# Small results of the first graph layer: one PSUM bank taken once, its halves handed out in turn

## The chip, the cores and the metric

The kernel runs on one core of a Trainium2 chip. The metric is the device time of one execution in microseconds. The engines are TensorE (PE in the profile, its weight loads PEld), VectorE (DVE), ScalarE (ACT), GpSimd (POOL) and SyncE (SP). PSUM, the memory into which TensorE writes, has eight banks of 128 partitions by 512 numbers of 4 bytes.

## The reference

Four layers work on x, 6250 nodes by 256, each with a layer norm ahead of it and a residual around it. The change lies in the first, a graph layer over 106250 edges that come sorted by their target:

```python
def _L0_gnn_ref(x, edge_index, edge_attr, u, batch, W1, b1, W2, b2):
    row, col = (edge_index[0], edge_index[1])
    h = jnp.concatenate([x[row], edge_attr], axis=1)
    h = jax.nn.relu(h @ W1 + b1)
    agg = jax.ops.segment_sum(h, col, num_segments=N_NODES)
    cnt = jax.ops.segment_sum(jnp.ones((h.shape[0],), h.dtype), col, num_segments=N_NODES)
    agg = agg / jnp.maximum(cnt, 1.0)[:, None]
    out = jnp.concatenate([x, agg], axis=1)
    return jax.nn.relu(out @ W2 + b2)
...
x = x + _L0_gnn_ref(_layernorm(x, axis=-1), edge_index, edge_attr_256, ...)
x = x + _L0_ffn_ref(_layernorm(x, axis=-1)[None], ...)[0]   # graph attention, then experts
x = x + _L1_gnn_ref(_layernorm(x, axis=-1), edge_weight, ...)
x = x + _L1_ffn_ref(_layernorm(x, axis=-1)[None], ...)
```

For each edge the hidden vector is relu(x[source] W1a + attribute W1b + b1). Each node takes the mean of its edges' hidden vectors, multiplies itself and the mean with W2, and adds the result to x.

## The kernel before

**Tiling.** The nodes stand in 49 blocks of 128 (`w`), seven blocks to a batch. As the edges are sorted by target, a block's edges are a window of consecutive ones. A window is worked on in three groups (`NG`) of six chunks (`G1`) of 128 edges, so the first layer's main loop runs over 147 groups `q`.

**Ahead of the loop** the product x W1a + b1 of every node is written to DRAM (`y_dram`), so that an edge only needs the row of its source. The layer's keys for a sort that the last graph layer wants, and the index windows of later batches, are made beside the loop.

**A group.** `load_sources(q)` has GpSimd gather the six chunks' rows of `y_dram` into a ring of four buffers `h` (L1128). `load_attr` fetches the attributes `ea` (L1399), and `turn` transposes them on VectorE into `et` (L1490). `hidden(q, j)` has TensorE multiply two chunks of `et` by `w1b` into `ph` (L1115, 128 x 1536 numbers, three banks). `join(q)` adds `ph` to the gathered rows on VectorE (L1508) and takes the relu on ScalarE (L1509). `add_up(q)` sums the edges per node: a 0/1 matrix `eq` (L1225) times `h`, accumulated over the window's three groups in `pe` (L1523, L1531), with a column of ones that counts the edges.

**The end of a block** is the generator `end_of(w)`. It is put in the list `work` once the block's last group has been summed, and each call of `steps` lets it go on to its next `yield`. In order:

- the count is inverted and the mean `ag` (a tile `o`) evicted from `pe` (L1541, L1542, L1544);
- `transposed` turns `ag` with two transposes by TensorE into a small PSUM tile `pt` (L1109) and evicts it on ScalarE (L1110);
- four Matmults with `w2` fill the next `pt` (`pm`; L1115, `pt<-w,b_all` and `pt<-w,o`), and VectorE adds the bias (L1556) and updates `x_all`, with the layer norm's statistics behind it;
- ScalarE writes the normed rows `xn` (L1572; also a tile `o`), which are turned in the same way into `b_all`;
- two Matmults with `wgx` give 24 numbers for each node (`pg`, `pt<-wgx,b_all`), the scores and values of the next layer, which ScalarE evicts in three pieces: `gtab` (L1583, L1584) and `a_dst` (L1585).

**Order.** Within one round of the loop the order is written out by hand, and `Ordered.pin()` keeps every engine's instructions in program order:

```python
if 0 < q <= NQ1: join(q - 1)
if q < NQ1: hidden(q, 0)
steps(sort)
if q >= 2: add_up(q - 2)   # every third q: work.append(end_of(...))
...                        # load_sources(q + 2), turn(q + 1)
if q < NQ1: hidden(q, 2)
steps()
if q < NQ1: equals[q] = equal(...); hidden(q, 4)
steps(slow)
```

So `steps` is called three times in a round, and nine times in a block. `end_of` has eleven pieces: the score product of block w comes one call ahead of the transposes of block w+1's mean, with the two chunks of one `hidden` (four Matmults) between them.

**PSUM.** Two buffers of `ph` take six banks, `pe` takes one, and the pool `p1`, with one buffer, the last. Every small result of the loop takes the tile `pt` of that pool: the four of `end_of`, the totals of `find_starts` (L1035), the two index transposes of `load_windows` (L1153), and in `sorted_edges` five transposes of keys (L1322), whose tile is [P, 4, P]. The three helpers get the pool as an argument and only call its `tile`. Which instruction must wait for which is worked out from the tiles' addresses and the pool's reuse when the program is built; the semaphores are put in there.

Of the kernel before, what the change touches and what calls it, by code (L numbers as in the profile page):

```python
# [1 line left out]

# [6 lines left out]
F32 = mybir.dt.float32  # L9
# [4 lines left out]
PSUM = bass.MemoryType.PSUM  # L14
DRAM = bass.MemoryType.DRAM

P = 128
# [4 lines left out]
def spread(n):  # L22

    cuts = [n] if n % 16 == 0 else [n // 16 * 16, n]
    return list(zip([0, *cuts[:-1]], cuts))


class Ordered:

    def __init__(self, tc):  # L30
        self.tc, self.last = tc, {}
        self.traced = tc.nc.cur_bb.bb.instructions
        self.at = self.traced[-1]
# [22 lines left out]
def general_path(ctx: ExitStack, tc: tile.TileContext, a: dict, out: bass.AP):  # L56
# [75 lines left out]
    def node_parts(ap, t0, t1):  # L132

        full = ap[0 : FULL * T, :].rearrange("(p t) d -> p t d", t=T)
        for p0, p1 in spread(FULL):
            yield slice(p0, p1), slice(t0, t1), full[p0:p1, t0:t1, :]
        if REST > t0:
            t2 = min(t1, REST)
            rest = ap[FULL * T + t0 : FULL * T + t2, :].rearrange("(o t) d -> o t d", o=1)
            yield slice(FULL, FULL + 1), slice(t0, t2), rest  # L140
# [728 lines left out]
def kernel(ctx: ExitStack, tc: tile.TileContext, a: dict, out: bass.AP):  # L869
# [10 lines left out]
    N, D = a["x"].shape  # L880
# [51 lines left out]
    def near_blocks(g):  # L932

        k = g * G + G / 2
        mid = k * (N / KM) / P
        spread_of = (C2 * (k / C2) * (1 - k / C2)) ** 0.5 * (N / KM) / P
        n = min(NK, int(-(-2 * (4.2 * spread_of + 0.9) // 1)))
        b0 = min(max(round(mid - n / 2), 0), T - 2)
        return b0, min(max(round(mid - n / 2) + n, b0 + 2), T) - b0
# [4 lines left out]
    with ExitStack() as fast:  # L944
# [51 lines left out]
        if T1 > C1:  # L996
            V.memset(flat.bitcast(I32)[:, C1:T1], 2**24)
            n = E1 - C1 * P
# [50 lines left out]
        def node_parts(ap, t0, t1):  # L1049

            t2 = min(t1, T - 1)
            if t2 > t0:
                rows = ap[t0 * P : t2 * P, :].rearrange("(t p) d -> p t d", p=P)
                yield slice(0, P), slice(t0, t2), rows
            if t1 == T:
                for p0, p1 in spread(LAST):
                    rows = ap[(T - 1) * P + p0 : (T - 1) * P + p1, :]
                    yield slice(p0, p1), slice(T - 1, T), rows.rearrange("p (o d) -> p o d", o=1)
# [248 lines left out]
        def sorted_edges(pst, wk):  # L1307

            k = order.bitcast(I32)[:, 0:KT]
            V.tensor_scalar(src2, k[:, 0:KA], 8191, None, op0=OP.bitwise_and)  # L1310
            some = key[:, 0:KT]
            for v, s in ((high, 20), (low, 13)):
                vi = some.bitcast(I32)
                V.tensor_scalar(
                    vi, k, s, 127, op0=OP.logical_shift_right, op1=OP.bitwise_and
                )
                V.tensor_copy(some, vi)
                V.tensor_scalar(some, some, -1.0, 127.0, op0=OP.mult, op1=OP.add)
                V.tensor_copy(v, some)
            for c in range(KA // P):  # L1320
                pt = pst.tile([P, 4, P], F32, name="pt")
                TE.transpose(pt[:, 0, :], some[:, c * P : (c + 1) * P], ident)  # L1322
                lt = wk.tile([P, P], BF16, name="lt")
                SC.activation(lt, pt[:, 0, :], AF.Copy)
                SC.dma_start(low_dram[c * P : (c + 1) * P, :], lt)
            V.tensor_add(good2[:, 1:2], good3[:, 0, 0:1], good3[:, 1, 0:1])
            V.tensor_add(good2[:, 3:4], good3[:, 0, 1:2], good3[:, 1, 1:2])

            lim = key[:, 0:KA]
            for g in range(KA // G):  # L1330
                V.memset(lim[:, g * G : (g + 1) * G], float(near_blocks(g)[0]))
            hit = order[:, 0:KA]
            V.tensor_tensor(hit, high[:, 0:KA], lim, op=OP.is_ge)
            for g in range(KA // G):
                V.memset(lim[:, g * G : (g + 1) * G], sum(near_blocks(g)) - 0.5)
            V.tensor_tensor(lim, lim, high[:, 0:KA], op=OP.is_ge)
            V.tensor_mul(hit, hit, lim)
            V.tensor_reduce(good2[:, 0:1], hit, axis=AX.X, op=OP.add)
# [5 lines left out]
        with ExitStack() as layer:  # L1344
# [114 lines left out]
            with (  # L1459
# [1 line left out]
                tc.tile_pool(name="y0", bufs=1) as wy,  # L1461
                tc.tile_pool(name="ph1", bufs=2, space=PSUM) as psh,
                tc.tile_pool(name="pe1", bufs=1, space=PSUM) as pse,
                tc.tile_pool(name="p1", bufs=1, space=PSUM) as psm,
            ):

                ring = [wy.tile([P, G1, HS], F32, name=f"h{i}") for i in range(4)]
                for h in ring:
                    V.memset(h[:, :, D:WS], 1.0)
# [134 lines left out]
                def sorting():  # L1604

                    yield from sort_steps()
                    sorted_edges(psm, wk)
# [151 lines left out]
        with (  # L1759
# [484 lines left out]
            k = NA + 5  # L2244
# [14 lines left out]
        with (  # L2259
# [297 lines left out]
            k = 0  # L2557
# [21 lines left out]
        with (  # L2579
# [6 lines left out]
            n = wk.tile([P, NB + 7], F32, name="n")  # L2586
# [4 lines left out]
            for i in range(2):  # L2591
                k = NB + 1 + 2 * i
# [55 lines left out]
```

## Time and profile before

| | |
|---|---|
| three runs | 4157.3, 4181.16, 4193.34 us; median 4181.16 |
| the profiled execution's own time | 4184.73 us |
| its span | 4182.9 us |
| granted TensorE clock, mean over the span | 0.857 |
| TensorE busy | 3303.4 us, 79% of the span |
| VectorE, GpSimd, ScalarE busy | 51%, 54%, 27% |

The profile shows one execution. Its times are microseconds from the span's start unless marked ns. "Idle before" is the time in which an engine stood ahead of an instruction, and the name behind the arrow is what ended it: an engine and line, a DMA, "issue" (it waited for nothing that the profile shows) or "remote" (an event that can't be tied to an instruction of this core). A float32 Matmult of the program stands in the trace as two records.

### The profile page before, as it was taken

The numbers are of one execution on the slowest core, as the hardware profiler recorded it, in microseconds if no ns is written. First come the engines' busy times: TensorE is split into PE (matmuls) and PEld (weight loads), VectorE is DVE, ScalarE is ACT, GpSimd is POOL, SyncE is SP. The second block draws the span as 40 slices with busy tenths as digits, with TensorE's granted clock in tenths as the row PEclk, the third lists the DMA queues.
The fourth block names the chain that finished last, engine by engine and source line by source line (L and its number), as shares of the span: only waits on it lengthen the run. The fifth ranks groups of instructions, "written<-read, shape, count | busy, mean of one in ns | idle before, by whom it ended". The sixth has DMA issues, their size and how long they took to land.

```text
span 4182.9 us, 57093 instructions
## 1 busy us (share of the span) xinstructions
PE 3303.4 (79%) x18509; PEld 2578.7 (62%) x18509; DVE 2138.8 (51%) x5571; ACT 1127.3 (27%) x2014; POOL 2249.3 (54%) x2364
## 2 busy tenths in 40 slices
PE   6888888898898885888898998786256866767788
PEld 5566666666576664677787777674245544555566
DVE  6566566665554444656455657555223333333344
ACT  4122222222222222333434344452001211111123
POOL 0656556566565634455454545534666666666651
PEclk8899999999899997999999999896557677767778
DMA  5677777777676742323333334333111111111210
GB/s 174 158 176 167 163 168 168 162 169 163 154 176 164 168 109 53 82 66 89 88 81 101 97 85 111 72 77 95 44 47 49 51 50 49 51 49 51 53 50 20
DMA packets 699200, 428.56 MB, mean 102 GB/s; under 512 B 531305, under 2 KB 640348, under 8 KB 698893
## 3 DMA queue, kind: packets, MB, share of 16 engines
q0 software_dynamic: 89408, 178.08, 18.4%
q1 hardware_dynamic: 366236, 187.21, 16.9%
q10 hardware_dynamic: 243248, 59.52, 7.2%
q8 instruction: 150, 2.46, 0.3%
q14 instruction: 158, 1.29, 0.1%
HBM read 382.05 MB, written 42.49 MB: 101 GB/s over the span
## 4 chain that ended last, share of the span: by engine, by line
PE 50%; another core or an unknown queue 18%; DVE 7%; issue 6%; ACT 3%; DMA 1%; POOL 0%; SPq 0%; ACTq 0%; DVEq 0%
PE ph L1115 22%; PE py L1115 10%; PE pe L2513 5%; PE pt L1115 4%; PE po L1873 4%; PE pe L1531 3%; PE pa L1810 1%; DVE eq L2492 1%; PE pt L1109 1%; DMA rb<-low_dram 1%; ACT hh L1709 1%; PE pe L2508 1%; ACT L1709 0%; DVE x_all L2054 0%
## 5 line engine op out<-in xcount | busy, mean ns | idle before, releaser
L1128 POOL DMA_INDIRECT h<-y_dram,src x882 | 846.6, 960 | 666.5 <-issue 508.4
L1128 POOL DMA_INDIRECT hg<-hp_dram,src x831 | 785.7, 946 | 457.8 <-issue 229.1
L1128 POOL DMA_INDIRECT sg<-gat_dram,src x640 | 612.0, 956 | 623.0 <-DVE px L1845 339.0
L1115 PE MATMUL ph<-w1b,et 128*128 128x256 f32 x3528 | 863.3, 397 | 35.9 <-issue 25.7
L1115 PEld LDWEIGHTS ph<-w1b,et 128*128 128x128 f32 x3528 | 677.5, 197 | 205.3 <-issue 115.9
L2513 PE MATMUL pe<-eq,hg 128*128 128x96 f32 (+15 forms) x2036 | 372.6, 331 | 158.3 <-issue 100.6
L2513 PEld LDWEIGHTS pe<-eq,hg 128*128 128x128 f32 x2036 | 359.0, 250 | 224.9 <-issue 157.8
L1508 DVE TENSOR_TENSOR h<-ph,h 128x1536 f32<-128x1536 f32 x147 | 258.2, 1757 | 428.8 <-remote 149.4
L1115 PE MATMUL py<-w,hh 128*128 128x256 f32 x1568 | 408.4, 400 | 64.2 <-ACT hh L1709 33.7
L1115 PE MATMUL ph<-b_all,w 128*128 128x256 f32 (+1 forms) x1600 | 417.1, 400 | 11.3 <-issue 9.8
L2492 DVE TENSOR_SCALAR eq<-px,dst,ew 128x96 f32<-128x96 f32 x831 | 262.3, 372 | 319.3 <-remote 137.4
L1509 ACT ACTIVATE h<-h 128x1536 f32<-128x1536 f32 x147 | 218.2, 1485 | 725.4 <-DMA ea<-in_edge_attr_dram 293.2
L1115 PEld LDWEIGHTS py<-w,hh 128*128 128x128 f32 x1568 | 300.3, 199 | 118.1 <-ACT hh L1709 41.7
L1115 PEld LDWEIGHTS ph<-b_all,w 128*128 128x128 f32 x1600 | 307.8, 202 | 55.4 <-issue 16.6
L1531 PE MATMUL pe<-h,eq 128*32 128x257 f32 x3168 | 257.2, 412 | 41.2 <-issue 40.9
L1873 PE MATMUL po<-pp,B 128*128 128x240 f32 (+10 forms) x1280 | 261.1, 344 | 17.2 <-DVE acc L1879 7.1
L1709 ACT ACTIVATE hh<-ph,b 128x256 f32<-128x256 f32 (+1 forms) x400 | 165.7, 466 | 392.0 <-remote 151.0
L1490 DVE STREAM_TRANSPOSE et<-ea 128x1536 f32<-128x1536 f32 x147 | 260.5, 1773 | 13.1 <-issue 9.5
L1873 PEld LDWEIGHTS po<-pp,B 128*128 128x128 f32 x1280 | 220.4, 194 | 32.0 <-issue 8.4
L1531 PEld LDWEIGHTS pe<-h,eq 128*32 128x32 f32 x3168 | 106.1, 115 | 148.0 <-issue 100.9
L1115 PE MATMUL py<-ew,g 65*128 65x256 f32 x392 | 136.5, 474 | 68.2 <-DVE x_all L2468 58.2
L1852 DVE TENSOR_TENSOR pp<-px,A 128x960 f32<-128x960 f32 (+10 forms) x160 | 156.3, 977 | 39.9 <-remote 27.5
(339 smaller groups left out, 3808.8 us busy)
## 6 DMA issues: line engine op xcount, KB each, us to landing
ea<-in_edge_attr_dram ACTq DMA_DIRECT2D x588, 96.0 KB
ea<-in_edge_attr_dram SPq DMA_DIRECT2D x588, 96.0 KB
y<-y SPq DMA_DIRECT2D x196, 128.0 KB
w<-in_L_ffn_W_dram SPq DMA_DIRECT2D x48, 512.0 KB
y<-ys SPq DMA_DIRECT2D x96, 256.0 KB
rb<-low_dram SPq DMA_DIRECT2D x80, 256.0 KB
h<-y_dram,src POOLq DMA_INDIRECT x882
hg<-hp_dram,src POOLq DMA_INDIRECT x831
```

The source lines that it names most:

```text
L1109: TE.transpose(pt[:, c, :], src[:, c * P : (c + 1) * P], ident)
L1115: TE.matmul(dst, lhs(c), rhs(c), start=c == 0, stop=c == n - 1)
L1128: GP.indirect_dma_start(out=dst, out_offset=None, in_=table[0:NP, :], in_offset=IndirectOffsetOnAxis(ap=idx, axis=0),)
L1490: V.transpose(et[q].rearrange("p c m k -> p m c k"), ahead.pop(q).rearrange("p i m (c k) -> p (i m) c k", c=2),)
L1508: V.tensor_add(h, ph.pop(q), h)
L1509: SC.activation(h, h, AF.Relu)
L1531: TE.matmul(sums[w][b * Q : (b + 1) * Q, :], eq[k][:, j, at], h[:, i * NT + j, 0:WS], start=g == 0 and j == NT - 1, stop=g == last_of[b] a ...
L1709: SC.activation(hidden[u][:, f, :n, :], ph[:, f - f0, :n, :], AF.Gelu, bias=b1[:, e, f : f + 1],)
L1852: V.tensor_tensor(pps[g, half][:, :, 0:n, :], pay[:, js, :].unsqueeze(2).to_broadcast([P, HG, n, HV]), near[g][:, js, 0:n].unsqueeze(3).to ...
L1873: TE.matmul(po.rearrange("p b v -> p (b v)"), B[:, j, :], pp[:, j, 0:n, :].rearrange("p b v -> p (b v)"), start=half == 0 and j == 0, stop ...
L2492: V.tensor_scalar(equals[k][:, j, :], lanes[:, 0:NW], dst_of[:, t : t + 1], ew[:, t : t + 1], op0=OP.is_equal, op1=OP.mult,)
L2513: TE.matmul(sums[b][:, lo - t0 * P : hi - t0 * P], hg[:, j, :], eq[:, j, lo - n0 : hi - n0], start=False, stop=after >= (t0 + n) * P,)
```

## The change

The pool `p1` gets the name `pends`. A new class `Halves` takes one tile of that pool, [P, 2, 256], and stands in for it as `psm`. Its `tile` hands out the first half, the second, the first again, and so on. A request for more than 256 numbers for each partition would get the whole bank. For no request to be so long, the tile of `sorted_edges` goes from [P, 4, P] to [P, 2, P]. All lines behind it move down by 18 or 19, so L1109 becomes L1127.

```diff
+class Halves:
+
+    def __init__(self, pool, width):
+        self.width, self.last = width, 1
+        self.bank = pool.tile([P, 2, width], F32, name="pt")
+
+    def tile(self, shape, dtype, name):
+        n = math.prod(shape[1:])
+        assert dtype == F32 and n <= 2 * self.width
+        if n > self.width:
+            v = self.bank.rearrange("p a k -> p (a k)")[:, 0:n]
+        else:
+            self.last = 1 - self.last
+            v = self.bank[:, self.last, 0:n]
+        return v if len(shape) == 2 else v.rearrange("p (c k) -> p c k", c=shape[1])
...
-                pt = pst.tile([P, 4, P], F32, name="pt")
+                pt = pst.tile([P, 2, P], F32, name="pt")
                 TE.transpose(pt[:, 0, :], some[:, c * P : (c + 1) * P], ident)
...
                 tc.tile_pool(name="ph1", bufs=2, space=PSUM) as psh,
                 tc.tile_pool(name="pe1", bufs=1, space=PSUM) as pse,
-                tc.tile_pool(name="p1", bufs=1, space=PSUM) as psm,
+                tc.tile_pool(name="p1", bufs=1, space=PSUM) as pends,
             ):
 
+                psm = Halves(pends, D)
                 ring = [wy.tile([P, G1, HS], F32, name=f"h{i}") for i in range(4)]
```

More of the change, by code (lines that the diff above doesn't have):

```diff
@@ L1 @@
+import math
 from contextlib import ExitStack
```

## The prediction

> **What bounds the kernel now.** I read the page's chain of waits first, then the table of stretches, then, for the first layer alone, TensorE's groups of instructions, the waits of all engines, and last the timeline around one of the places where TensorE stands.
>
> ```profile
> ## 4 chain that ended last, share of the span: by engine, by line
> PE 50%; another core or an unknown queue 18%; DVE 7%; issue 6%; ACT 3%; DMA 1%; POOL 0%; SPq 0%; ACTq 0%; DVEq 0%
> ```
>
> ```profile
> core 0: us, PE busy (x) PEld busy (x) DVE busy (x) ACT busy (x) POOL busy (x), PEclk, DMA share, GB/s
> 0.00:150.00 150.00, 103.39 (x441) 75.21 (x442) 92.39 (x309) 47.53 (x111) 30.55 (x39) 0.86 0.63 170
> 150.00:1540.00 1390.00, 1203.10 (x7395) 898.79 (x7394) 802.89 (x1556) 317.69 (x530) 816.73 (x851) 0.93 0.72 163
> ...
> ```
>
> The changed lines run in the second stretch: 1390.00 us of a span of 4182.9. There TensorE (PE) is busy 1203.10 us, 87%, at a granted clock of 0.93; no other engine reaches 60%. So the first layer is bound by TensorE, and a change to buffers can touch only the 187 us in which it stands. Half of the whole chain is TensorE's work, and the second entry, 18%, is time ended by an event that the trace can't tie to an instruction; the same word ("remote") comes back in the rows below.
>
> ```profile
> line engine op names shapes xcount | busy us, mean ns | idle before us <-releasers
> L1115 PE MATMUL ph<-w1b,et 128*128 128x256 f32 x3435 | 837.8, 395 | 26.3 <-issue 25.7
> L1531 PE MATMUL pe<-h,eq 128*32 128x257 f32 x3120 | 250.6, 411 | 31.6 <-issue 31.3
> ...
> L1109 PE MATMUL pt<-ident,o 128*128 128x128 f32 x192 | 40.8, 297 | 81.0 <-remote 47.5 <-ACT a_dst L1585 24.1 <-issue 4.2
> L1115 PE MATMUL pt<-wgx,b_all 128*128 128x24 f32 x188 | 26.1, 258 | 21.8 <-DVE dst L1170 10.6 <-issue 7.0 <-ACT b_all L1110 1.6
> ```
>
> The figures behind the bar are TensorE's idle time just ahead of the group. The largest, 81.0 us, stands ahead of the transposes into the bank of small results, which the change divides. Two entries make up most of it:
>
> ```profile
> PE pt L1109 <- remote: 47.5, 8, 9.2
> ...
> PE pt L1109 <- ACT a_dst L1585: 24.1, 4, 8.6
> ```
>
> That is 71.6 us in 12 places of 4 to 9 us. They are transposes of the mean of block w+1, and a_dst is ScalarE's last read of block w's score product from the same bank. One of the 12 in the timeline:
>
> ```profile
> 1482.89 0.52 PE L1115 MATMUL pt<-wgx,b_all 128*128 128x24 f32 x4
> ...
> 1483.26 1.97 PE L1115 MATMUL ph<-w1b,et 128*128 128x256 f32 x8
> ...
> 1493.25 0.18 ACT L1583 ACTIVATE gtab<-pt 128x16 f32<-128x16 f32 x1 [11.89 <-remote]
> 1493.33 0.17 ACT L1584 ACTIVATE gtab<-pt 128x4 f32<-128x4 f32 x1
> 1493.38 0.18 ACT L1585 ACTIVATE a_dst<-pt 128x4 f32<-128x4 f32 x1
> 1493.62 0.29 PEld L1109 LDWEIGHTS pt<-ident,o 128*128 128x128 f32 x2 [8.79 <-issue]
> 1493.62 0.69 PE L1109 MATMUL pt<-ident,o 128*128 128x128 f32 x2 [8.39 <-remote]
> ```
>
> The score product (wgx) ends at 1483.4, TensorE goes on with two chunks of the hidden product (ph) until 1485.2, then stands until 1493.6. ScalarE was free all that time (11.89 us idle), and began only at 1493.25, although what it reads was written 9.8 us before. The three evictions take half a microsecond. So what is late is not the eviction but the news that the product is finished. In the other 36 of 48 blocks that news is quick, the evictions are done under the 1.7 to 2.0 us of the ph Matmults, and the transposes begin 0.22 us after the preceding ph record: no loss.
>
> **The change part by part.** Built, both programs have the same instructions in the same order on every engine (10693 rows on TensorE, 9889 on VectorE, 5012 on ScalarE, 4419 on GpSimd, 2386 on SyncE) and the same transfers, so no Matmult, eviction or DMA is added, removed or moved past a queue. Only addresses in the bank and semaphore waits differ:
>
> (a) TensorE's waits for ScalarE, VectorE and DMAs are the same before and after, instruction by instruction. The transposes of block w+1 write the other half now, and yet they still wait for a_dst of block w: the program that arranges the waits keeps this one by bank. So the wait that ends last in the 12 places stays. Saving: 0.
>
> (b) 48 first transposes lose a wait of TensorE for its own wgx product (a separate instruction of the sequencer, for which the trace's rows of L1109 give 51 ns each). In the stalled places this instruction is stamped 1493.257 to 1493.308, and the transposes' weights load at 1493.62, after a_dst ends at 1493.56: the self-wait ends first and a_dst decides. Gain between 0 and 48 x 0.051 = 2.4 us; I take 0, because in 36 of 48 places the sequencer runs ahead under ph.
>
> (c) 95 first Matmults of a group (ph, L1115 before) and 7 of the sums (pe) gain a wait of TensorE for its own work, 17 to 34 Matmults back. In all there are 43 more such waits, as some replace others: 43 x 0.051 = 2.2 us if all were exposed. Could they stand? The trace has the same kind: 49 ph Matmults already carry one; in 48 of these 49 the Matmult begins 0.22 us after the one ahead, as without a wait, and once 3.2 us pass. By that row 102 more cost at most 102 x 3.2 / 49 = 6.7 us, at least 0. Queued behind such a wait is the rest of the group's ph product, for which VectorE's join (L1508) waits, and behind that ScalarE's relu and the sums; work so far back is as a rule long finished (at most 16 Matmults were recorded between a product and the instruction that it woke). I take +1.
>
> (d) The sort's five key transposes take a tile half as long (only one of its four columns was ever used), and the eviction waits on VectorE and ScalarE are merged with others that TensorE's wait implied: nothing is queued behind them that was not before. 0.
>
> Sum: between -2.4 and 2.2 + 6.7 = +8.9; taken +1. The profiled execution took 4184.73 us (span 4182.9 and 1.83 around it) and goes to about 4186. It lies 3.6 above the median of the runs shown, 4181.16, so the median goes to 4182.
>
> If the 12 late completions came at other moments, the transposes' 81.0 would change by themselves: one more place of 6 us is 0.15% of the time.
>
> The Trainium skill, "PSUM — Partial Sum Buffer", section "PSUM bank collisions raise a hardware error", speaks against the change: engines sharing PSUM are to be held apart by bank and quadrant, not by address, so two halves of one bank count as one place. By that rule the gain is 0, as under (a); were halves independent, the 71.6 us would be free, and the sum 4110. No run here shows a collision.
>
> **The rivals.** Faster: the stalls ahead of the transposes vanish, because TensorE's wait for itself is what holds back the news of its finished work (both disappear at the same moment, 1493.25), and without it ScalarE is told at once. For it: the product is finished, ScalarE idle, and both waits are for one event. Against: late news is also seen where TensorE waits for nothing of its own, in later layers. Price: 71.6 us, or the 47.5 alone: 4110 to 4134.
>
> Slower: the same idea, on the other side. The 95 ph waits put a self-wait into groups that had none, and the news of the product before them, which the join L1508 awaits, comes late. Among joins that TensorE's completion woke, those with a self-waiting ph behind the product learned of it 2.88 us late on average (over 4 us in 7 of 28), those with self-waiting transposes behind it 2.76 us (7 of 16), those with a plain pm product behind it 0.98 us (0 of 25). After the change 48 groups trade transposes for ph, an even exchange; 47 groups go from the third kind to the first: 47 x (2.88 - 0.98) = 89 us, if TensorE bears all of it, and 45 if the two ph buffers absorb half: 4226 to 4270. This decides from the point where a join begins so late that the second ph buffer isn't free when its next group begins. Against it: the three kinds stand at different places of a block, with different transfers around, and 48 of 49 existing waits cost nothing visible on TensorE itself.
>
> That the change doesn't do what it says (halves used in turn, but waited for as one) is my main case.
>
> **How the numbers follow.** Main case 0.57, at 4182; its own range is the runs' spread with the sum's ends, 4155 to 4202. Faster rival 0.17, slower rival 0.26, because its counts of 7 and 0 are harder to call chance than the one coincidence in time behind the faster. The range of 8 in 10 reaches into both: 4120 to 4250. Over 1% (42 us, about what a measurement of this kernel can tell from no change) faster 0.17, within 0.57, slower 0.26.
>
> **What would show it.** In the profile after: the transposes (L1127 then) with some 70 to 90 us of idle time, the a_dst entry among its releasers, no self-wait at that line, and a first layer within 20 us of 1390. The faster rival shows under 30 us there and a first layer near 1320; the slower one more idle time ahead of ph and the sums, and longer "remote" waits of the join than its 134.7 us now. A first layer changed by over 40 us with the same waits, or a change outside it, would make my reading wrong.

## The result, and the profile after

The changed kernel took 4184.52 us (median of 21 runs), the kernel before 4179.2 beside it (21 runs): ratio 1.0007, 95% interval 0.9989 to 1.0024. Nothing changed that this measurement could tell. The profiled execution after took 4191.95 us with a span of 4190.2.

The table of stretches of the changed kernel, first layer (columns as before: the stretch, its length, busy time of TensorE, its weight loads, VectorE, ScalarE, GpSimd, the granted clock, the DMA share, GB/s):

```profile
150.00:1540.00 1390.00, 1193.89 (x7363) 893.50 (x7363) 798.16 (x1546) 314.39 (x526) 817.79 (x851) 0.92 0.72 163
```

A fixed stretch says nothing of the layer's length, only how full it is. The length can be read from the 49 rows of a_dst, one for each block: from the first to the last went 191.4 to 1553.9 us before (1362.5) and 190.9 to 1564.4 after (1373.5). The 11 us more are within what the runs of either kernel differ by (4157 to 4203 before, 4169 to 4210 after).

TensorE's groups in that stretch, with the idle time ahead of each behind the bar:

```profile
L1133 PE MATMUL ph<-w1b,et 128*128 128x256 f32 x3431 | 833.9, 395 | 21.6 <-issue 20.9 <-PE ph L1133 0.4
L1550 PE MATMUL pe<-h,eq 128*32 128x257 f32 x3120 | 248.2, 412 | 24.4 <-issue 23.8 <-DMA h<-y_dram,src 0.4
...
L1127 PE MATMUL pt<-ident,o 128*128 128x128 f32 x190 | 41.0, 301 | 105.0 <-issue 51.7 <-ACT a_dst L1604 44.0 <-DVE start L1054 8.8
```

The idle time ahead of the transposes is still the largest, 105.0 us (81.0 before), and a_dst is still among what ended it. Ahead of ph and of the sums pe, where the new self-waits are, it is no longer than before (21.6 and 24.4, against 26.3 and 31.6). That the waits moved as the programs said is seen from the waits' own records, of the transposes' line first and of the products' line second (54 and 53 before; the line of the sums has 47, before 40, so there are 43 more in all):

```profile
L1127 PEldq EVENT_SEMAPHORE  x7: 51/51/51, 235.1 to 933.3; - x7
```

```profile
L1133 PEldq EVENT_SEMAPHORE  x136: 51/51/6386, 154.0 to 1537.3; - x136
```

And one stalled place of the changed kernel in the timeline:

```profile
1206.74 0.52 PE L1133 MATMUL pt<-wgx,b_all 128*128 128x24 f32 x4
...
1207.11 1.97 PE L1133 MATMUL ph<-w1b,et 128*128 128x256 f32 x8
...
1218.70 0.18 ACT L1602 ACTIVATE gtab<-pt 128x16 f32<-128x16 f32 x1 [13.34 <-remote]
1218.79 0.17 ACT L1603 ACTIVATE gtab<-pt 128x4 f32<-128x4 f32 x1
1218.84 0.18 ACT L1604 ACTIVATE a_dst<-pt 128x4 f32<-128x4 f32 x1
1219.07 0.29 PEld L1127 LDWEIGHTS pt<-ident,o 128*128 128x128 f32 x2 [10.39 <-ACT a_dst L1604]
1219.07 0.69 PE L1127 MATMUL pt<-ident,o 128*128 128x128 f32 x2 [9.99 <-ACT a_dst L1604]
```

It is the picture of before without the self-wait: the score product is done at 1207.3, ScalarE waits 13.34 us and reads it only at 1218.70, and the transposes into the other half load 0.37 us later, as they did before (1493.25 and 1493.62). The ph Matmults behind the score product, which now carry the self-wait, begin at 1207.11 without a pause; what TensorE stands in is the wait for a_dst, behind late news of the score product.

### The profile page after: what moved, and what is told of

The parts are those of the page before. It is cut to its first block, busy times and chain, and to the rows that moved or that the text cites. A ratio compares the mean times of both kernels' runs of the same rounds, so it can differ in the third digit from the quotient of the medians.

```text
span 4190.2 us, 57139 instructions
## 1 busy us (share of the span) xinstructions
PE 3318.1 (79%) x18509; PEld 2591.1 (62%) x18509; DVE 2138.2 (51%) x5571; ACT 1127.4 (27%) x2014; POOL 2247.6 (54%) x2364
## 4 chain that ended last, share of the span: by engine, by line
PE 37%; another core or an unknown queue 10%; issue 6%; DVE 5%; ACT 3%; POOL 2%; DMA 1%; SPq 0%; DVEq 0%; ACTq 0%; POOLq 0%
PE ph L1133 12%; PE py L1133 10%; PE pe L2532 5%; PE po L1892 4%; PE pt L1133 2%; POOL hg L1146 2%; PE pa L1829 1%; ACT hh L1728 1%; DVE eq L2511 1%; DMA rb<-low_dram 1%; ACT L1728 1%; PE pe L2527 0%; DVE x_all L2487 0%; PE pt L1127 0%
## 5 line engine op out<-in xcount | busy, mean ns | idle before, releaser
L1133 PE MATMUL py<-w,hh 128*128 128x256 f32 x1568 | 419.9, 408 | 73.4 <-ACT hh L1728 38.8
```

The source lines that it names most:

```text
L1133: TE.matmul(dst, lhs(c), rhs(c), start=c == 0, stop=c == n - 1)
```

## The experiments

The theory: the halves are waited for as one bank, so ScalarE's last read still ends the stalls, and TensorE's waits for itself cost nothing. Against it stood that the self-waits themselves make the news late (with either sign, or cancelling), that halves are independent, and that a stall taken away here comes back at the next wait.

One thing must be said ahead of all numbers: the same kernel before took 3436.6 and 3438.3 us beside the kernels of the first and third group below, and 4241.6 beside those of the second; the three groups ran on three different chips. So only ratios within a group are compared.

**Does the last read end the stalls? No reading of the product.** The three evictions take their input from SBUF:

```diff
-SC.activation(gtab[:, w, 0:HX], pg[:, 0:HX], AF.Copy)
+SC.activation(gtab[:, w, 0:HX], x_all[:, w, 0:HX], AF.Copy)
...  # the same for the other two
```

> Left out: the three evictions at the end of a block no longer read the score product from PSUM; they read the block's node rows from SBUF instead (the scores of the next layer are therefore others; instruction count and order are unchanged). So ScalarE has nothing to wait for, and the next block's transposes are free of the a_dst wait; TensorE's 48 waits for its own score product stay. Theory (the a_dst wait kept by bank is what ends the stalls): idle time ahead of the transposes falls from 81 us to under 25, first layer about 50 to 70 us shorter, total 4110 to 4130. Rival 1 (TensorE's wait for itself holds the news back): the stalls stay at 70 to 100 us, total 4165 to 4195. Rival 2 (the late news is met at the next wait instead): idle ahead of the transposes falls, but idle ahead of ph, pe or pt elsewhere rises by as much; total within 20 us of before.

Measured: 3427.94 us against 3436.62, ratio 0.9978 (0.9967 to 0.9989). None of the three forecasts could be told apart, because on this chip there was hardly a stall left to remove. The stretch from 150 to 1400 us, kernel without the read (its last a_dst starts at 1293.1, so the end of the stretch is the next layer's):

```profile
150.00:1400.00 1250.00, 1224.67 (x8187) 960.42 (x8186) 881.01 (x1774) 367.31 (x629) 883.27 (x925) 0.99 0.87 189
```

TensorE is busy 98% instead of 87%; up to 1290 us, within the layer, it is 1118.2 of 1140 us, 98% too. I compared, for the VectorE and ScalarE instructions that wait for TensorE's completion, the end of the Matmult with the start of the waiting instruction: between 150 and 1540 us none of some 600 was over 1 us late, while in the profile of before 87 of 488 were, by 360 us in all. The late news was absent here with other kernels too: the control below, which keeps the evictions' read and the bank of before, is as full.

**Real separation: two banks, and its control.** In the control `split_6`, ph becomes six one-bank buffers of two chunks each, and the join three additions; in `split_5_2` one of the six banks goes to the small results:

```diff
-tc.tile_pool(name="ph1", bufs=2, space=PSUM) as psh,
+tc.tile_pool(name="ph1", bufs=5, space=PSUM) as psh,   # control: 6
-tc.tile_pool(name="p1", bufs=1, space=PSUM) as psm,
+tc.tile_pool(name="p1", bufs=2, space=PSUM) as psm,    # control: 1
...
-if j == 0:
-    ph[q] = psh.tile([P, G1, D], F32, name="ph")
+ph[q, j] = psh.tile([P, 2, D], F32, name="ph")
...
-V.tensor_add(h, ph.pop(q), h)
+for j in range(0, G1, 2):
+    V.tensor_add(h[:, j : j + 2, :], ph.pop((q, j)), h[:, j : j + 2, :])
```

> Control for the next kernel: ph as six one-bank buffers of two chunks each instead of two buffers of three banks; the join on VectorE is three additions of 128 x 512 instead of one of 128 x 1536. Waits between blocks are as before. All theories: same time within 20 us, unless the earlier start of a third of the join helps (up to 20 us faster); stalls ahead of the transposes 70 to 105 us as before.

> As the control, but with five one-bank buffers of ph and a second real bank for the small results, so that the wait of block w+1's transposes for a_dst of block w is gone from the program, and the output is complete. Theory: 40 to 70 us under the control, idle ahead of the transposes under 25 us. Rival (late news met at the next wait): within 20 us of the control, with the idle time found ahead of ph or the product with w2 instead.

Measured: 0.9970 (0.9955 to 0.9985) for the control, 0.9961 (0.9948 to 0.9974) for two banks. The 10 us of the control came as allowed for; the second bank's 40 to 70 us did not, for the same reason as above: the control, for which 70 to 105 us ahead of the transposes were expected, had 3.2 us there. TensorE's row of the stretch, control first, two banks second:

```profile
150.00:1400.00 1250.00, 1224.67 (x8187) 958.93 (x8186) 908.36 (x2058) 368.06 (x632) 885.44 (x926) 0.99 0.92 189
```

```profile
150.00:1400.00 1250.00, 1224.17 (x8196) 960.52 (x8196) 909.87 (x2062) 367.64 (x632) 884.36 (x926) 0.99 0.93 189
```

Both are at 98%, so a second bank has at most some 25 us in this stretch to win.

**Do the gathers make the news late?**

```diff
-gather(rows_of(q)[:, j, 0:D], y_dram, src1[:, w, k, t : t + 1])
+GP.dma_start(out=rows_of(q)[:, j, 0:D], in_=y_dram[w * P : w * P + P, :])
```

> Left out: the gather. The six chunks of a group are fetched by plain transfers of 128 consecutive rows, issued by GpSimd in the same places (the edges get wrong sources). If the late news of TensorE's finished work comes from the gathers' packets (they are denser in the late spells), the remote waits of the join (134.7 us, 23 times) and of gtab (117.8 us, 12 times) fall to under a third and the first layer gets 60 to 150 us shorter, total 4030 to 4120. If it does not, the remote waits stay within 30% and the layer changes by less than 40 us, apart from what the join no longer waits for a late gather.

Measured: 1.001 (0.9999 to 1.0021). With no late news on the chip there was nothing to test; the run shows only that gathering is not what the layer's time is made of there (GpSimd's busy time in the stretch fell from 885 us, in the control, to 507, and the time stayed).

**Lateness made by design.** To be independent of the chip's own lateness, the second group puts a known delay on ScalarE ahead of the three evictions, in the kernel before, in the changed one and in the one with two banks. With them ran the changed kernel once more.

```diff
+spare = wy.tile([P, D], F32, name="spare")
...
+for _ in range(16):
+    SC.activation(spare, x_all[:, w, :], AF.Copy)
 SC.activation(gtab[:, w, 0:HX], pg[:, 0:HX], AF.Copy)
```

> The changed kernel once more, beside the kernel before on the same chip. Theory (same instructions, same cross-engine waits, 43 more waits of TensorE for work long done): within 0.3% of before in either direction, whatever the level of times. Rival (a gain from the self-wait taken from the transposes and a loss from those put at ph cancelled each other only by chance): where TensorE's news comes without delay neither exists, so the ratio would stay near 1 too, but where it comes late it would move by over 0.5% from run to run of the comparison.

> The kernel before, with sixteen copies of 128 x 256 numbers from SBUF to an unused tile put on ScalarE ahead of the three evictions of each block's scores (some 0.36 us each, 5.8 us in all), so that the last read of the small bank is late by design, as it was by the late news. All theories: TensorE stands ahead of the next block's transposes, for 49 x (5.8 - 1.7 of cover) = about 200 us, less what the sums' relu loses or the start of the copies gains: 100 to 250 us slower than before.

> The same sixteen copies in the changed kernel, where the evictions read one half and the transposes write the other. Theory (the halves are waited for as one bank): as slow as the previous kernel, within 20 us. Rival (halves are independent): 100 us or more faster than the previous kernel.

> The same sixteen copies with two real banks for the small results (five one-bank buffers of ph, three additions for the join). Theory: the transposes need not wait for the late evictions, so most of the loss of the two previous kernels is gone, 100 us or more faster than they are; what is left over the kernel without copies is ScalarE's own lateness elsewhere (relu, other evictions). Rival (lateness moves to the next wait): within 40 us of the two previous kernels.

Measured, beside 4241.61 us of the kernel before:

| kernel | median us | ratio to before (95%) |
|---|---|---|
| changed kernel again | 4246.04 | 1.0011 (0.998 to 1.0041) |
| before, with copies | 4367.87 | 1.0297 (1.026 to 1.0334) |
| changed, with copies | 4370.48 | 1.0296 (1.0259 to 1.0333) |
| two banks, with copies | 4259.77 | 1.0046 (1.0026 to 1.0066) |

This settles the question of the change. With the same delay the kernel before takes 126 us more, and the changed one 129 us more than the kernel before (124 more than its own run without copies): the halves hide nothing of it. The two-bank kernel with copies stands 18 us over the kernel before. That isn't the price of its copies, since this kernel was not run without them on that chip, and its join is in three parts, for which no control with copies was run; what the second bank itself does is read from the wait. TensorE's idle time ahead of the transposes from 150 to 1540 us, in the same order:

```profile
L1109 PE MATMUL pt<-ident,o 128*128 128x128 f32 x178 | 46.7, 354 | 226.1 <-issue 77.1 <-DMA h<-y_dram,src 72.8 <-ACT a_dst L1588 71.1
```

```profile
L1127 PE MATMUL pt<-ident,o 128*128 128x128 f32 x178 | 46.7, 354 | 222.5 <-DMA h<-y_dram,src 98.8 <-ACT a_dst L1607 63.6 <-issue 57.0
```

```profile
L1109 PE MATMUL pt<-ident,o 128*128 128x128 f32 x190 | 38.6, 287 | 17.3 <-issue 9.0 <-ACT o L1573 6.4 <-ACT lt L1324 1.5
```

The first two differ by 3.6 us, and in the third a_dst is no longer among the releasers. The changed kernel without copies had this row on that chip:

```profile
L1127 PE MATMUL pt<-ident,o 128*128 128x128 f32 x188 | 40.2, 299 | 102.6 <-ACT a_dst L1604 56.0 <-issue 40.5 <-ACT gtab L1603 5.5
```

With copies the layer is longer than this stretch. Up to 1700 us the rows read 251.7 us (before, with copies), 247.8 (changed, with copies), 20.6 (two banks, with copies) and 102.6 (changed, without). So with copies the changed kernel stands 145 us longer ahead of its transposes, now in some 50 places, mostly of about 5 us. Not all of that is time lost: ahead of TensorE's other large groups (ph, pe, the products with w2 and wgx) the changed kernel's idle time falls from 94 us to 17. From the first row of a_dst to the last go 1389.2 us in the changed kernel without copies, 1478.8 with them, 1482.6 in the kernel before with them, and 1390.6 with two banks and copies. "DMA h" and "issue" as releasers are the inference's: a wait for several events is put down to the one that came last by the records. A place where the last event can be seen, changed kernel with copies:

```profile
1023.60 0.52 PE L1133 MATMUL pt<-wgx,b_all 128*128 128x24 f32 x4
...
1023.96 1.97 PE L1133 MATMUL ph<-w1b,et 128*128 128x256 f32 x8
...
1024.34 7.12 ACT L1604 ACTIVATE spare<-x_all 128x256 f32<-128x256 f32 x16
...
1031.37 0.17 ACT L1605 ACTIVATE gtab<-pt 128x16 f32<-128x16 f32 x1
...
1031.49 0.18 ACT L1607 ACTIVATE a_dst<-pt 128x4 f32<-128x4 f32 x1
1031.71 0.29 PEld L1127 LDWEIGHTS pt<-ident,o 128*128 128x128 f32 x2 [6.18 <-ACT a_dst L1607]
1031.71 0.69 PE L1127 MATMUL pt<-ident,o 128*128 128x128 f32 x2 [5.78 <-ACT a_dst L1607]
```

The copies don't wait for the score product, so their start says nothing of its news; but the first eviction follows the last copy without a pause, so the news was there by then, and the delay alone holds the evictions. The transposes write one half, the evictions read the other, and TensorE waits 5.78 us for them. The copies took 7.12 us, not the 5.8 I had reckoned from an eviction's 0.36; 49 x (7.12 - 1.7) would be 266 us of standing. The 248 and 252 of the whole layer come near that. Some 103 us stood there already without copies, for the late news; as the total is no more than the delay's own, the late news must in large part have passed while the copies ran.

In the kernel with two banks not all is gone:

```profile
L1115 PE MATMUL pt<-w,o 128*128 128x256 f32 x188 | 66.8, 489 | 72.1 <-issue 46.0 <-ACT h L1510 13.7 <-ACT o L1110 12.5
```

72.1 us of idle time stand ahead of the second pair of w2 Matmults, whose operand is the mean that ScalarE, busier now, evicts. The changed kernel without copies had 3.1 us there. That is the lateness elsewhere that the expectation named.

**The first group's kernels once more.** In the hope of late news, four were run again, beside 3438.3 us of the kernel before.

> The kernel whose three evictions read the node rows instead of the score product, once more (the scores of the next layer are others). On a chip where the kernel before takes about 3440 us (TensorE stands for nearly nothing in the first layer): again 5 to 12 us faster. On one where it takes 4180 to 4240 us: theory (the a_dst wait ends the stalls), idle time ahead of the transposes under 25 us and 50 to 75 us faster in all; rival (TensorE's own wait, still there in 48 places, holds the news back), stalls of 70 to 100 us stay and the time is within 20 us of before; rival (the late news is met at the next wait), the stalls go from there but the time is within 20 us of before all the same.

> The control with six one-bank buffers of ph and one bank for small results, once more. Where the kernel before takes about 3440 us: again some 10 us faster. Where it takes 4180 to 4240: stalls ahead of the transposes 70 to 110 us as before, total within 30 us of before (the join in three parts can begin earlier).

> Five one-bank buffers of ph and two real banks for small results, once more. Where the kernel before takes about 3440 us: 1 to 5 us under the control. Where it takes 4180 to 4240: theory, 40 to 75 us under the control, idle time ahead of the transposes under 25 us; rival (late news met at the next wait), within 20 us of the control.

> The kernel with plain transfers of consecutive rows in place of the gather in the first layer (the edges get wrong sources), once more. Where the kernel before takes about 3440 us: within 0.3%, as measured. Where it takes 4180 to 4240: if the gathers' packets make the news of finished work late, the remote waits of the join (143 to 135 us) and of gtab (118 to 140 us) fall to under a third and the time by 50 to 150 us; if the lateness comes from elsewhere, they stay within 30% and the time within 40 us.

Measured: 0.9966 (0.9954 to 0.9978) without the read, 0.9972 (0.9959 to 0.9984) for the control, 0.9966 (0.9953 to 0.9978) for two banks, 1.0022 (1.0008 to 1.0036) without the gather. The branch with late news wasn't met, and its forecasts stay untested. Where news is prompt, the two-bank kernel is 0.39% and 0.34% under before, and its control 0.30% and 0.28%, with intervals that overlap: most of the gain is that of the divided ph and the join in three parts, and none is shown for the bank.

## Why the prediction was right, point by point

**The sum.** +1 us was taken, -2.4 to +8.9 bounded; the ratio 1.0007 is +3 us with an interval of -5 to +10, and 1.0011 on the second chip (+5, -8 to +17). Both hold the sum, but neither could tell its ends from 0. That the time fell into the range says little, as 4120 to 4250 was wide enough for half of either rival; what the prediction stands on is which wait ends the stalls.

**(a), the wait that stays,** is shown: with the last read late by design, the changed kernel loses what the kernel before loses, and with two real banks the transposes no longer wait for that read. My value of 71.6 us for independent halves was not measured where news is late by itself. As a bound from another side, the two-bank kernel with copies had 17.3 us ahead of the transposes where the changed kernel without copies had 102.6, 85 us less; but that is idle time at one place, and ahead of the second pair of w2 Matmults it had 69 us more.

The rule of the Trainium skill, "PSUM — Partial Sum Buffer", section "PSUM bank collisions raise a hardware error", that engines are held apart by bank and not by address, fits what the runs show of the waits. Whether the hardware would bear a read and a write in two halves of a bank at once is not shown: in all kernels here the wait forbade it, and leaving it out was not tried.

**(b), the self-wait taken away,** brought nothing that can be seen: in the stalled place after, the distance from the first eviction to the transposes' load is the same 0.37 us, and ScalarE's waits for late news are as many and as long (gtab waited 117.7 us in 12 "remote" places, against 117.8 in 12).

**(c), the self-waits put in:** 136 waits at the products' line in place of 53, and 43 more in all, as reckoned; idle time ahead of ph was lower by 4.7 us and of the sums by 7.2. No cost is seen, and the bound of 6.7 us held.

**The two rivals** rested on one idea, that a self-wait holds back the news. After the change these transposes have none, TensorE stands in its wait for ScalarE, and the news of the score product is as late; this ends the faster one. That a gain and a loss cancelled would have had to happen twice, at +0.07% and +0.11% on chips with late news. For the slower one the joins can be counted again, by what stands behind the product they wait for:

| behind the product | before | after | after, second chip |
|---|---|---|---|
| ph | 28 joins, 2.88 us late, 7 over 4 us | 27, 1.67, 3 | 26, 2.18, 4 |
| score product, then transposes | 16, 2.76, 7 | 23, 3.02, 8 | 19, 3.77, 7 |
| product with w2 | 25, 0.98, 0 | 30, 0.88, 1 | 26, 0.69, 0 |

The third kind got its self-wait behind it and stayed prompt. So the counts of 7 and 0 that gave this rival 0.26 belonged to the place in the block, not to the wait: I had compared places, not waits. The chance was too high, and with it the upper end of the range.

**What I had said the profile would show:** the first layer within 20 us (11 by the a_dst rows), a_dst among the releasers and the self-waits gone from the transposes but for 7, where I had forecast none. The idle time of 105.0 us lies above my 70 to 90. The changed kernel had 102.6 on another chip too, and the kernel before only one profile where news is late; whether its 81.0 was a low draw or the change moved some 20 us there from other places isn't shown. The time bounds what it can be in all: +3 us, -5 to +10.

**What stays open** is where the late news comes from. It is not the change, and not the kernel alone, since kernels that differ from it in single places have none of it on the two quick chips. The gathers alone don't make it, as they ran on the quick chips too, with prompt news; whether they do where news is late, no run could judge. Nor can the trace tell late news from a product that was itself finished late: the ends of Matmults in it are modelled, and "late" means here that the waiting engine started long after that end.

## What to carry to other kernels

Dividing this buffer gave nothing, since the program that places the waits saw one bank: compare the built programs' waits across engines before believing in a divided one, and if they are the same, forecast no change. When a buffer is suspected, make its reader late by a known amount in both versions; that gave 126 and 129 us where the plain times differed by 0.1%, and with two banks a stall of 21 us in place of 250. A wait that stands beside a stall isn't its cause for that; ask which of the two ends last.

## What the runs showed of the hardware that was not expected

The same kernel took 3437 us on two chips and 4179 to 4242 elsewhere. The granted clock of the kernel without the read was 0.99 in the first layer, against 0.92 to 0.93 in the two profiles of before and after, but the larger part in this layer is TensorE's idle time. From the first row of a_dst to the last the layer took 1362.5 us before, with TensorE busy for 1180.5, and 1129.9 without the read on the quicker chip, busy for 1108.1: of 233 us less, 160 are idle time and 72 quicker Matmults. With it goes the news of finished Matmults: at one place ScalarE started 11.4 us after the product it needed, and 87 of 488 such wake-ups were over 1 us late in the profile of before, none of some 600 on the quicker chip. That the late news makes the idle time is argued from this, not shown by a run that takes it away on one chip. Either way the 187 us that I took for the kernel's own slack were largely absent on another chip.
